# Three moves in the first part of a graph kernel: a check, a graph's split rows, and the turn of a state

## The chip, the core and the metric

The kernel runs on one core of one Trainium2 chip. The metric is the device time of one launch in microseconds (us). The engines are TensorE (PE in the profile; its weight loads are PEld), VectorE (DVE), ScalarE (ACT), GpSimd (POOL) and SyncE (SP), which here only issues DMAs. Each engine takes its own instructions in the order in which the program gives them, and waits on semaphores for the others.

## The reference

There are 16 graphs of 1024 nodes with 128 features. Two networks run one after the other; the change is in the part that computes the first network and, beside it, the adjacency of the second.

```python
# first network: four gated layers
h = x
for i in range(4):
    m = einsum('bjn,bjd->bnd', adj, h @ weight[i])
    gx, gh = m @ w_ih.T + b_ih, h @ w_hh.T + b_hh
    r = sigmoid(xr + hr); z = sigmoid(xz + hz); n = tanh(xn + r * hn)
    h = (1 - z) * n + z * h
x = layernorm(x + h * mask)

# second network: rows of adj are thinned one after the other
def step(carry, n):                  # for n = 0 .. 1023
    row = carry[n]
    num, rank = sum(row), cumsum(row)
    sf = where(num > 10, (num + 1) // 2, 1)
    rm = row & (rank % sf == 0)      # if num > 1
    carry[n] = row & ~rm
    carry[:, n] = carry[:, n] & ~rm  # later rows see it
# then three aggregations with adj * keep, batch norms, a head, layernorm
```

## The kernel before

The first part of the program (up to about 1470 us of 2624) holds two classes, whose instructions are woven into each other by hand: on PE, DVE, ACT, POOL and SP the order is that of the Python program.

`Gated` computes the first network. Two streams take turns, each with a graph of its own: stream 0 does a layer of its graph, then stream 1 a layer of its own, so that there are 64 layers in all. The state h lies turned, with features on partitions and the 1024 nodes along a row (`st.ht`, tile `h_h`), in two halves f = 0 and 1 of 512 nodes. A layer (`layer`, L1059) first aggregates: for each half 8 products with the high part of h by rows (`h_hi`) and 8 with the low part (`h_lo`), L1072, whose sum ScalarE copies to `h_ms` (L1075). Then come the gates of half 0 and half 1, all products at L1084. For each half: the reset gate's product, its sigmoid to `h_r` (L1093), the product ph, DVE's `(ph + b) * r` (L1099), the product px, DVE's sum (L1101), tanh (L1102), the update gate's product, its sigmoid to `h_z` (L1105), GpSimd's `z * h` (L1107), DVE's `(z - 1) * r` (L1108) and GpSimd's new half of h (L1109). The products rotate through five PSUM banks.

While one stream is in its layer, the other's new h is turned into rows for its next layer. `next_layer(f)` turns a half by four transposes into the tile `h_tr` (L1023), which has one PSUM buffer, and ScalarE copies that to `h_hi` (L1011); `rest(f)` subtracts on VectorE, from `h_tr` again, for `h_lo` (L1016). At a change of graph, `finish(f)` takes the place of this: it turns the half, ScalarE scales it (L1053), GpSimd adds it to x (L1055), and after the second half the sum is stored (L1057). `begin_rows` splits the next graph's x into `h_hi` on ScalarE (L1042) and `h_lo` on GpSimd (L1043, two of 512), and `begin` turns x (L1035).

`FixPoint` computes the thinning, in 32 blocks of 128 rows of four graphs. A block with index k cuts the columns that earlier blocks removed (`turn`, transposes at L722; `keep`, L727), ranks each row by a scan (`count`, L735), and takes the removals inside its diagonal by rounds. A round computes the row's parameters from the count (`params`, L694 to L701, six small DVE instructions into `f_q`), |scale * rank + bias| on ScalarE (`diag_u`, L886, four of 128) and the removals on VectorE (`removed`, L893, four, into `f_x`); `less` (L901 on PE, L903 on DVE) then gives the ranks without them, and the next round begins. After two such rounds `settle` computes ranks and parameters a third time, `wide_u` (ScalarE, L909 and L912) and `rows` (DVE, L863) write the four rows of 1024 and store them, and load the row of a later block. `last_u` and `check` do the diagonal a third time: `check` takes `removed` of it, four L893 from `f_u` in SBUF, and compares (L879) it with the round before. The result of the comparison goes into `bad`, which is looked at only at the end of the program.

`FixPoint.steps` is a generator of 20 places a block, and a layer takes ten of them: `aside(n)`, made by `beside` (L1141), runs the next place and then the jobs of the other stream that are listed under n. So a block lasts two layers. Places 0 to 3 stand in the aggregation and 4 behind it; 5 and 6 belong to half 0, 7, 8 and 9 to half 1. In the layers of stream 0 place 4 holds the fourth turn, keep and count, the first parameters and `diag_u`, and then `check` of the block before (L812); place 5 holds `removed`, 7 holds `less` with parameters and `diag_u`, 8 the second `removed`. In those of stream 1, places 1 to 4 hold `settle`, `wide_u` and `rows`, 5 the mask `f_both` (L775, four on VectorE and one on GpSimd) and the first turn, 6 the first count, 8 and 9 the second. `last_u` is handed back by place 4 and runs behind the first sigmoid.

The lines that say where the places stand in a half:

```python
nc.scalar.activation(r, pr, AF.Sigmoid, bias=bias(self.bs, 0))
if f == 1:
    aside(7)
elif later:
    later()
...
nc.scalar.activation(r, r, AF.Tanh, bias=bias(self.bi, 2))
aside(5 if f == 0 else 8)
```

Of the kernel before, what the change touches and what calls it, by code (L numbers as in the profile page):

```python
# [8 lines left out]
F32 = mybir.dt.float32  # L9
BF = mybir.dt.bfloat16  # L10
F16 = mybir.dt.float16
# [10 lines left out]
P = 128  # L22
# [604 lines left out]
class FixPoint:  # L627
# [17 lines left out]
    G = 4  # L645
# [40 lines left out]
    def params(self, num, r, rd=None):  # L686

        nc, G = self.nc, self.G
        q = self.small.tile([P, 4, G], F32, name="f_q")
        t = self.small.tile([P, 2, G], F32, name="f_t")  # L690
        h = self.sm[:, 2, r, :]
        ts, stt = nc.vector.tensor_scalar, nc.vector.scalar_tensor_tensor

        ts(h, num, 0.25 + 2.0 ** -14, HALVES, op0=ALU.mult, op1=ALU.add)  # L694
        ts(t[:, 1, :], num, 10.5, -3.0, op0=ALU.is_gt, op1=ALU.mult)
        ts(q[:, 0, :], num, 10.5, 1.0, op0=ALU.is_gt, op1=ALU.mult)
        stt(q[:, 1, :], h, HALVES, t[:, 1, :], op0=ALU.subtract, op1=ALU.mult)
        if rd:
            rd()
        stt(t[:, 0, :], h, HALVES, q[:, 0, :], op0=ALU.subtract, op1=ALU.mult)  # L700
        stt(q[:, 2, :], num, 1.5, t[:, 0, :], op0=ALU.is_le, op1=ALU.max)  # L701
        return q
# [34 lines left out]

    def steps(self):

        nc, G = self.nc, self.G
        for c in range(G):
            self.load(c)
        old = None
        for i, (k, b0) in enumerate(self.todo):
            diag = slice(k * P, k * P + P)

            yield  # L750
            if old:
                old.settle()
                old.wide_u(0)
            yield
            if old:
                old.wide_u(1)
                old.rows(0)
            yield
            if old:
                old.wide_u(2)  # L760
                old.rows(1)
            yield
            if old:
                old.rows(2)
                old.wide_u(3)
                old.rows(3)
            a = [self.loaded.pop((i, g)) for g in range(G)]
            pt = self.ps.tile([P, G, P], F32, name="f_pd")
            for g in range(G):
                nc.tensor.transpose(pt[:, g, :], a[g][:, diag], self.cst["ident"])  # L770
            yield old and old.last_u

            both = self.small.tile([P, G, P], BF, name="f_both")
            for g in range(G):
                nc.vector.tensor_mul(both[:, g, :], a[g][:, diag], pt[:, g, :])  # L775
            nc.gpsimd.affine_select(both, both, pattern=[[0, G], [1, P]], compare_op=ALU.is_gt, fill=0.0,
                                    base=0, channel_multiplier=-1)
            self.turn(i, 0)
            yield
            rank = self.two.tile([P, G, N], F16, name="f_rank")  # L780
            self.keep(i, a[0])
            self.count(i, 0, a[0], rank, pt)
            yield
            yield
            self.turn(i, 1)
            self.keep(i, a[1])
            yield
            self.count(i, 1, a[1], rank, pt)
            if i == 0:

                for c in range(G, self.LOTS):
                    self.load(c, nc.scalar)
            yield
            yield
            yield
            self.turn(i, 2)
            self.keep(i, a[2])
            self.count(i, 2, a[2], rank, pt)
            yield
            for g in range(G):  # L800
                self.read_back(i + 1, g)
            yield
            self.turn(i, 3)
            self.keep(i, a[3])
            self.count(i, 3, a[3], rank, pt)

            num = self.sm[:, 0, 0, :]
            nc.vector.tensor_scalar(num, rank[:, :, N - 1], 1.0, None, op0=ALU.mult)
            q = self.params(num, 0)
            u = self.diag_u(rank[:, :, diag], q)  # L810
            if old:
                old.check()  # L812
            yield
            x = self.removed(u, q, both)
            yield
            yield
            pd, num = self.less(x, rank, 1)
            rd = self.small.tile([P, G, P], F16, name="f_rd")
            q = self.params(num, 1, lambda: nc.vector.tensor_sub(rd, rank[:, :, diag], pd))
            u = self.diag_u(rd, q)  # L820
            yield
            x = self.removed(u, q, both)
            yield
            old = self.Block(self, i, a, rank, both, x)
            yield
        yield
        old.settle()
        for n in range(4):
            old.wide_u(n)
            if n < 3:  # L830
                yield
            old.rows(n)
        yield old.last_u
        yield
        old.check()

# [51 lines left out]
        return u  # L888

    def removed(self, u, q, both):  # L890
        x = self.small.tile([P, self.G, P], BF, name="f_x", bufs=3)
        for g in range(self.G):
            self.nc.vector.scalar_tensor_tensor(x[:, g, :], u[:, g, :], q[:, 2, g:g + 1], both[:, g, :],  # L893
                                                op0=ALU.is_equal, op1=ALU.mult)
        return x
# [21 lines left out]
class Gated:  # L917
# [141 lines left out]
    def layer(self, st, l, aside):  # L1059
# [6 lines left out]
        for f in range(2):  # L1066
# [7 lines left out]
            m = wk.tile([C, HF], F32, name="h_ms")  # L1074
            nc.scalar.copy(m, pm[f])  # L1075
            ms.append(m)
        later = aside(4)
        bias = lambda t, g: t[:, 3 * l + g:3 * l + g + 1]
        w = lambda t, g: t[:, l, g, :]

# [6 lines left out]
        for f in range(2):  # L1087
            h, m = st.ht[:, half[f]], ms[f]
            r = wk.tile([C, HF], F32, name="h_r")
            z = wk.tile([C, HF], F32, name="h_z")  # L1090
            zh = wk.tile([C, HF], F32, name="h_zh")
            pr = gate((w(self.wh, 0), h), (w(self.wi, 0), m))
            nc.scalar.activation(r, pr, AF.Sigmoid, bias=bias(self.bs, 0))  # L1093
            if f == 1:
                aside(7)
            elif later:
                later()
            ph = gate((w(self.wh, 2), h))
            nc.vector.scalar_tensor_tensor(r, ph, bias(self.bh, 2), r, op0=ALU.add, op1=ALU.mult)  # L1099
            px = gate((w(self.wi, 2), m))  # L1100
            nc.vector.tensor_add(r, px, r)  # L1101
            nc.scalar.activation(r, r, AF.Tanh, bias=bias(self.bi, 2))  # L1102
            aside(5 if f == 0 else 8)
            pz = gate((w(self.wh, 1), h), (w(self.wi, 1), m))
            nc.scalar.activation(z, pz, AF.Sigmoid, bias=bias(self.bs, 1))  # L1105

            nc.gpsimd.tensor_tensor(zh, z, h, ALU.mult)  # L1107
            nc.vector.scalar_tensor_tensor(r, z, 1.0, r, op0=ALU.subtract, op1=ALU.mult)  # L1108
            nc.gpsimd.tensor_tensor(h, zh, r, ALU.subtract)  # L1109
            aside(6 if f == 0 else 9)  # L1110
# [30 lines left out]
    def beside(self, st, ot, l, s, b0, steps):  # L1141


        before = l if s == 0 else l + 1
        if before in (0, L0):
            old = not (s == 0 and b0 == 0)
            new = not (s == 1 and b0 + 2 >= B)
            jobs = {5: [], 7: [], 9: []}
            nxt = ot.b + 2 if old else ot.b

            def begin():
                ot.b = nxt
                ot.begin(0)

            if old:
                jobs[5].append(lambda: ot.finish(0))
                jobs[7].append(lambda: ot.finish(1))
                jobs[0] = [lambda: ot.load_x(nxt)]
                for j in range(4, NB):
                    jobs.setdefault(j // 2 - 2, []).append(lambda j=j: ot.load_adj(nxt, j))  # L1160
            if new:
                jobs.setdefault(3 if old else 0, []).append(lambda: ot.begin_rows(nxt))
                jobs[9].append(begin)
        else:
            jobs = {5: [lambda: ot.next_layer(0), lambda: ot.rest(0)],
                    7: [lambda: ot.next_layer(1)], 8: [lambda: ot.rest(1)]}

        if l == L0 - 1:

            for j in range(4):  # L1170
                jobs.setdefault(4, []).append(lambda j=j: st.load_adj(st.b + 2, j))

        def aside(n):
            if n == 8:
                for job in jobs.get(n, ()):
                    job()
            later = next(steps, None)
            if n != 8:
                for job in jobs.get(n, ()):
                    job()  # L1180
            return later
        return aside


# [789 lines left out]
```

## Time and profile before

| | us |
|---|---|
| median of 3 runs | 2628.1 |
| lowest and highest | 2625.91, 2628.13 |
| profiled execution | 2626.24 |
| its span, from first to last instruction | 2624.5 |

Some rows of the page's table of groups, which the text below draws on:

| line, engine, tile | count | busy us | mean ns of one |
|---|---|---|---|
| L1084 PE h_g from h_h and h_wh | 768 | 418.4 | 628 |
| L1072 PE h_g from h_a and h_hi | 1024 | 280.0 | 415 |
| L735 DVE f_rank | 128 | 299.2 | 2343 |
| L863 DVE f_nr | 128 | 164.7 | 1289 |
| L1107 POOL h_zh | 128 | 219.1 | 1712 |
| L1109 POOL h_h | 128 | 164.3 | 1284 |
| L1102 ACT tanh to h_r | 128 | 92.5 | 723 |

How to read the lines that follow. A row of a timeline has the start and the length in us, engine, line, operation, output from input, the shape, a count, and in brackets the idle time of the engine before it and what ended it. Matmuls are pipelined, so that a row of several is a little longer than the time to the next row. A row of the view of waits has who waited for whom, the total in us, the number of waits and the longest. A row of the view of stretches has the stretch, its length, the busy time of PE, PEld, DVE, ACT and POOL, the clock that TensorE was granted (1.00 is full), the DMA engines' share and GB/s. Spans on POOL are rough.

### The profile page before, as it was taken

Reading aid. Unit: us, or ns where it says so; the run is one execution under the profiler, and the core shown is the slowest. Engines: PE = TensorE matmul, PEld = TensorE weight load, DVE = VectorE, ACT = ScalarE, POOL = GpSimd, SP = SyncE. Lnnn points to the kernel's source line nnn. Section 1 sums busy time; section 2 is a strip of 40 time slices with the busy share of each in tenths; the row PEclk is TensorE's granted clock in tenths of the full one; section 3 lists DMA queues with packets and bytes.
Section 4 is the critical chain, followed back from the end, with each engine's and each line's share of the span. In section 5 each row is a group of like instructions: output and inputs, shape, how many; then the busy total and the mean of one; then the engine's idle time right before and its main releaser. Section 6 shows DMA issues by size and latency. Waiting matters only on the chain.

```text
span 2624.5 us, 36126 instructions
## 1 busy us (share of the span) xinstructions
PE 2362.3 (90%) x12167; PEld 1590.7 (61%) x12167; DVE 1908.1 (73%) x4116; ACT 1404.2 (54%) x3228; POOL 1005.9 (38%) x938
## 2 busy tenths in 40 slices
PE   5998999989989999989899599999999989998875
PEld 4555555555555555555555367777777767777654
DVE  4887877888868888878788666666666566665667
ACT  3555455556455555555554455555555435545647
POOL 3335244353253442433532455544554434441000
PEclk9999999999999999999999899999999989999988
DMA  7236253363252352523630677667667366655304
GB/s 237 103 103 221 66 186 121 104 211 117 90 192 87 129 201 65 204 98 105 210 121 23 229 257 256 228 258 259 255 231 260 113 218 237 233 197 161 115 17 130
DMA packets 214391, 436.20 MB, mean 166 GB/s; under 512 B 59570, under 2 KB 80724, under 8 KB 214196
## 3 DMA queue, kind: packets, MB, share of 16 engines
q1 hardware_dynamic: 186756, 345.96, 37.9%
q0 software_dynamic: 23040, 83.90, 9.3%
q10 hardware_dynamic: 4400, 3.95, 0.5%
q8 instruction: 98, 1.61, 0.2%
q14 instruction: 97, 0.79, 0.1%
HBM read 324.49 MB, written 109.25 MB: 165 GB/s over the span
## 4 chain that ended last, share of the span: by engine, by line
PE 49%; DVE 22%; ACT 15%; DMA 6%; issue 6%; POOL 1%; ACTq 0%; DVEq 0%; SPq 0%; POOLq 0%
PE h_g L1084 12%; PE h_g L1072 12%; PE p_ag L1519 6%; DVE f_rank L735 3%; ACT s_junk L1359 3%; PE q_ag L1748 2%; ACT f_pd L886 2%; DMA h_x<-in_x_dram 2%; PE q_ob L1712 2%; DVE s_r L1370 2%; DMA p_a<-in_adj_dram 2%; DVE h_r L1099 1%; DVE h_r L1101 1%; PE p_u L1434 1%; PE h_tr L1023 1%
## 5 line engine op out<-in xcount | busy, mean ns | idle before, releaser
L1084 PE MATMUL h_g<-h_h,h_wh 128*128 128x512 f32 x768 | 418.4, 628 | 5.7 <-ACT h_ms L1075 5.5
L1084 PE MATMUL h_g<-h_ms,h_wi 128*128 128x512 f32 x768 | 405.0, 610 | 0.0
L1107 POOL TENSOR_TENSOR h_zh<-h_z,h_h 128x512 f32<-128x512 f32 x128 | 219.1, 1712 | 482.4 <-ACT h_z L1105 482.3
L735 DVE TENSOR_TENSOR_SCAN f_rank<-f_a,f_first,f_pd 128x1024 f16<-128x1024 f32 x128 | 299.2, 2343 | 3.0
L1449 POOL CAST p_b<-p_at 128x512 uint8<-128x512 f32 x256 | 213.1, 853 | 204.5 <-ACT p_at L1442 189.3
L1072 PE MATMUL h_g<-h_a,h_hi 128*128 128x512 f32 x1024 | 280.0, 415 | 0.0
L1084 PEld LDWEIGHTS h_g<-h_ms,h_wi 128*128 128x128 f32 x768 | 152.7, 199 | 197.3 <-issue 194.0
L1072 PE MATMUL h_g<-h_a,h_lo 128*128 128x512 f32 x1024 | 256.9, 393 | 0.0
L1442 ACT ACTIVATE p_at<-p_u,s_less 128x512 fp32r<-128x512 f32 x256 | 175.4, 686 | 146.3 <-PE p_u L1441 127.9
L863 DVE SCALAR_TENSOR_TENSOR f_nr<-f_u,f_q,f_a 128x1024 bf16<-128x1024 f16 x128 | 164.7, 1289 | 90.4 <-ACT f_u L912 73.6
L1072 PEld LDWEIGHTS h_g<-h_a,h_hi 128*128 128x128 f32 x1024 | 188.3, 188 | 57.5 <-issue 20.6
L1072 PEld LDWEIGHTS h_g<-h_a,h_lo 128*128 128x128 f32 x1024 | 189.9, 188 | 38.8
L1102 ACT ACTIVATE h_r<-h_r,h_bi 128x512 f32<-128x512 f32 x128 | 92.5, 723 | 193.3 <-DVE h_r L1101 192.7
L1084 PEld LDWEIGHTS h_g<-h_h,h_wh 128*128 128x128 f32 x768 | 135.7, 201 | 96.4 <-issue 79.6
L1455 DVE SCALAR_TENSOR_TENSOR p_junk<-p_a 128x1024 bf16<-128x1024 f32 x128 | 184.2, 1439 | 2.3
L1359 ACT ACTIVATE s_junk<-s_o 128x128 bf16<-128x128 f32 x384 | 113.6, 298 | 132.7 <-DVE s_o L1352 132.7
L1109 POOL TENSOR_TENSOR h_h<-h_zh,h_r 128x512 f32<-128x512 f32 x128 | 164.3, 1284 | 16.5 <-DVE f_tr L903 4.3
L909 ACT ACTIVATE f_u<-f_rank,f_q 128x128 f16<-128x128 f16 (+7 forms) x128 | 110.6, 867 | 90.1 <-DVE f_rank L849 90.1
L1075 ACT COPY h_ms<-h_g 128x512 f32<-128x512 f32 x128 | 73.9, 577 | 140.9 <-PE h_g L1072 98.5
L1440 PE MATMUL p_u<-ident_b,p_a 128*128 128x128 bf16 x1024 | 143.8, 221 | 4.4 <-DMA p_a<-in_adj_dram 4.4
L1441 PE MATMUL p_u<-ident_b,p_nr 128*128 128x128 bf16 x1024 | 143.8, 221 | 0.0
L1108 DVE SCALAR_TENSOR_TENSOR h_r<-h_z,h_r 128x512 f32<-128x512 f32 x128 | 105.6, 825 | 49.3 <-ACT h_z L1105 47.9
(241 smaller groups left out, 4988.2 us busy)
## 6 DMA issues: line engine op xcount, KB each, us to landing
h_a<-in_adj_dram POOLq DMA_DIRECT2D x128, 512.0 KB, 7.2
p_a<-in_adj_dram SPq DMA_DIRECT2D x128, 512.0 KB
f_a<-in_adj_dram SPq DMA_DIRECT2D x124, 512.0 KB
e_nr<-f_nr SPq DMA_DIRECT2D x128, 256.0 KB
p_nr<-e_nr SPq DMA_DIRECT2D x32, 1024.0 KB
s_at<-p_b SPq DMA_DIRECT2D x32, 512.0 KB
s_ag<-s_ag SPq DMA_DIRECT2D x64, 256.0 KB
q_agi<-s_ag SPq DMA_DIRECT2D x32, 512.0 KB
```

The costliest lines, as they stand in the source:

```text
L735: nc.vector.tensor_tensor_scan(out, a, other[:, 0, 0:1].to_broadcast([P, N]), start, op0=ALU.add, op1=ALU.bypass)
L863: nc.vector.scalar_tensor_tensor(nr, self.us[g], self.q[:, 2, g:g + 1], self.a[g], op0=ALU.not_equal, op1=ALU.is_ge)
L1072: nc.tensor.matmul(pm[f], part[:, j, :], st.adj[j][:, half[f]], start=(j == 0 and n == 0), stop=(j == NB - 1 and n == 1))
L1084: nc.tensor.matmul(pg, lhs, rhs, start=(i == 0), stop=(i == len(mm) - 1))
L1107: nc.gpsimd.tensor_tensor(zh, z, h, ALU.mult)
L1109: nc.gpsimd.tensor_tensor(h, zh, r, ALU.subtract)
L1359: self.nc.scalar.activation(junk, o[:, i, :], AF.Square, accum_out=ss[:, i:i + 1])
L1440: nc.tensor.matmul(pu[:, i * P:(i + 1) * P], a[:, blk, 1], ib, start=False, stop=False)
L1442: nc.scalar.activation(g["at"][:, j, cols], pu, AF.Relu, bias=self.less2)
L1449: self.nc.gpsimd.tensor_copy(g["b", f][:, j, :], g["at"][:, j, f * HF:(f + 1) * HF].bitcast(F32))
L1455: self.nc.vector.scalar_tensor_tensor(junk, a, 0.0, a, op0=ALU.is_gt, op1=ALU.not_equal, accum_out=self.bad[:, c:c + 1])
L1519: self.nc.tensor.matmul(pa, hi[:, j, :], at[:, j, f * HF:(f + 1) * HF], start=(start and n == 0), stop=(stop and n == len(js) - 1))
```

## The change

There are three edits and what they need of buffers.

- `check` of the block before goes from place 4 of stream 0's layer to its last place, 9, ahead of the making of the new `Block`. What it reads must live longer: `f_q` gets three buffers, `f_x` four; `f_rd` gets one.
- Places and jobs of half 0: `aside(5)` moves from behind the tanh to behind the reset gate's sigmoid, where `later` and `aside(7)` stood. With it move the first `removed` (stream 0's layers), `f_both` and the first turn (stream 1's), and the turn of the other stream's h with the copy to `h_hi`, or at a change of graph `finish(0)`. The subtraction for `h_lo` stays behind the tanh, under the name "rest". `last_u` is called in place 5 itself.
- `begin_rows` of the next graph goes from place 3 to place 7, behind `finish(1)`.

```diff
-        q = self.small.tile([P, 4, G], F32, name="f_q")
+        q = self.small.tile([P, 4, G], F32, name="f_q", bufs=3)
...
-            yield old and old.last_u
+            yield
+            if old:
+                old.last_u()
...
             u = self.diag_u(rank[:, :, diag], q)
-            if old:
-                old.check()
             yield
...
-            rd = self.small.tile([P, G, P], F16, name="f_rd")
+            rd = self.small.tile([P, G, P], F16, name="f_rd", bufs=1)
...
             x = self.removed(u, q, both)
             yield
+            if old:
+                old.check()
             old = self.Block(self, i, a, rank, both, x)
...
-        x = self.small.tile([P, self.G, P], BF, name="f_x", bufs=3)
+        x = self.small.tile([P, self.G, P], BF, name="f_x", bufs=4)
...
             nc.scalar.activation(r, pr, AF.Sigmoid, bias=bias(self.bs, 0))
-            if f == 1:
-                aside(7)
-            elif later:
-                later()
+            aside(5 + 2 * f)
...
             nc.scalar.activation(r, r, AF.Tanh, bias=bias(self.bi, 2))
-            aside(5 if f == 0 else 8)
+            aside("rest" if f == 0 else 8)
...
-                jobs.setdefault(3 if old else 0, []).append(lambda: ot.begin_rows(nxt))
+                jobs.setdefault(7 if old else 0, []).append(lambda: ot.begin_rows(nxt))
...
-            jobs = {5: [lambda: ot.next_layer(0), lambda: ot.rest(0)],
+            jobs = {5: [lambda: ot.next_layer(0)], "rest": [lambda: ot.rest(0)],
                     7: [lambda: ot.next_layer(1)], 8: [lambda: ot.rest(1)]}
...
         def aside(n):
-            if n == 8:
-                for job in jobs.get(n, ()):
-                    job()
-            later = next(steps, None)
-            if n != 8:
-                for job in jobs.get(n, ()):
-                    job()
-            return later
+            if n not in ("rest", 8):
+                next(steps, None)
+            for job in jobs.get(n, ()):
+                job()
+            if n == 8:
+                next(steps, None)
```

More of the change, by code (lines that the diff above doesn't have):

```diff
@@ L832, in steps @@
             old.rows(n)
-        yield old.last_u
+        yield
+        old.last_u()
         yield
@@ L1076, in layer @@
             ms.append(m)
-        later = aside(4)
+        aside(4)
         bias = lambda t, g: t[:, 3 * l + g:3 * l + g + 1]
```

## The prediction

> **What bounds the kernel now.** I read the page first, for the engines and TensorE's clock.
>
> ```profile
> span 2624.5 us, 36126 instructions
> PE 2362.3 (90%) x12167; PEld 1590.7 (61%) x12167; DVE 1908.1 (73%) x4116; ACT 1404.2 (54%) x3228; POOL 1005.9 (38%) x938
> ```
>
> TensorE looks like the bound, but in the first part (46 to 1446 us) it is busy for 1289 us of 1400. So I asked next what it waits for, in the view of waits for TensorE from 100 to 1400 us (total, times, longest).
>
> ```profile
> PE f_pd L901 <- DVE f_x L893: 64.8, 35, 3.1
> PE h_tr L1023 <- DVE h_lo L1016: 15.7, 28, 0.6
> PE h_tr L1023 <- ACT h_w L1053: 11.0, 14, 1.4
> ```
>
> It waits for VectorE. Third, TensorE's timeline at such a place, and the granted clock behind it (the number after the engines' busy times):
>
> ```profile
> 453.87 0.38 PE L901 MATMUL f_pd<-f_tri,f_x 128*128 128x128 bf16 x4 [1.39 <-DVE f_x L893]
> 454.88 0.63 PE L1023 MATMUL h_tr<-ident,h_h 128*128 128x128 f32 x4 [0.63 <-DVE h_lo L1016]
> ```
>
> ```profile
> 456.00:457.00 1.00, 1.00 (x3) 0.47 (x2) 0.86 (x5) 0.30 (x1) 0.92 (x2) 0.50 0.00 0
> ```
>
> Reading that view in steps of 0.25 us, I find 25 such stretches of half clock, each 3.41 or 3.42 us long, so each costs 1.71 us of work; each follows a stretch of the same length in which TensorE idled about 2 us or more.
>
> Last, VectorE's timeline over one block, which decides the forecast:
>
> ```profile
> 490.67 0.17 DVE L808 TENSOR_SCALAR f_tr<-f_rank 128x4 f32<-128x4 f16 x1
> ...
> 491.62 1.13 DVE L893 SCALAR_TENSOR_TENSOR f_x<-f_u,f_q,f_both 128x128 bf16<-128x128 f16 x4
> 492.78 0.69 DVE L879 SCALAR_TENSOR_TENSOR f_junk<-f_x 128x512 f16<-128x512 bf16 x1
> 493.40 0.08 DVE L879 DVE_READ_ACCUMULATOR f_junk<-f_x 128x1 f32 x1
> 494.06 0.75 DVE L1099 SCALAR_TENSOR_TENSOR h_r<-h_g,h_bh,h_r 128x512 f32<-128x512 f32 x1 [0.57 <-ACT h_r L1093]
> 494.91 0.69 DVE L1101 TENSOR_TENSOR h_r<-h_g,h_r 128x512 f32<-128x512 f32 x1
> 495.52 1.11 DVE L893 SCALAR_TENSOR_TENSOR f_x<-f_pd,f_q,f_both 128x128 bf16<-128x128 f32 x4
> ...
> 503.65 1.42 DVE L1108 SCALAR_TENSOR_TENSOR h_r<-h_z,h_r 128x512 f32<-128x512 f32 x1
> 505.00 0.15 DVE L903 TENSOR_TENSOR f_tr<-f_rank,f_pd 128x4 f32<-128x4 f16 x1
> ```
>
> L808 follows the fourth rank scan (call its start E); the second L903 after it opens the settling of the block. The next L808 stands at 533.06. So the round is E to L903, 14.33 us, and L903 to the next E, 28.06. Over 30 rounds the first leg is 14.3 to 14.9 us in the 23 without a change of graph (14.3 without half clock) and 17.3 to 20.3 in the other seven; the second is 27.9 to 31.3. In the second leg VectorE waits only for ScalarE, whose work hangs on the same L903, except 0.47 us for h_hi and 0.17 for TensorE's f_tr. The check (L893 on f_u, and L879, 1.86 us) is free where it stands: after it VectorE still waits 0.57 us for the sigmoid. So VectorE with ScalarE is as tight a ring as TensorE.
>
> **The Trainium skill.** "TensorE: Matmul & The Clock Gate", Part 1, says that TensorE's clock halves after an idle window of about 3.4 us; the trace agrees on the length (3.41), but about 2 us idle of it suffices, and I use that. "SBUF — State Buffer", Who interferes with whom, says that a VectorE instruction with two SBUF inputs and a GpSimd instruction that reads SBUF exclude each other, whoever comes first. The trace agrees. Above, L1108 took 1.42 instead of 0.69 us because GpSimd's L1107 had begun at 503.25. And at the end of the first part the check happens to stand beside GpSimd's work:
>
> ```profile
> 1460.25 1.71 POOL L1107 TENSOR_TENSOR h_zh<-h_z,h_h 128x512 f32<-128x512 f32 x1
> ...
> 1460.76 4.23 DVE L893 SCALAR_TENSOR_TENSOR f_x<-f_u,f_q,f_both 128x128 bf16<-128x128 f16 x4
> 1462.04 1.27 POOL L1109 TENSOR_TENSOR h_h<-h_zh,h_r 128x512 f32<-128x512 f32 x1
> 1463.26 1.31 POOL L1055 TENSOR_TENSOR h_x<-h_x,h_w 128x512 f32<-128x512 f32 x1
> ...
> 1465.02 0.69 DVE L879 SCALAR_TENSOR_TENSOR f_junk<-f_x 128x512 f16<-128x512 bf16 x1
> ```
>
> Four products of 1.13 us took 4.23: one passes between two of GpSimd's instructions.
>
> **The change part by part**, in the block above, times from E.
>
> *f_x ahead of the gate.* diag_u runs from +0.80 to +2.74 (491.47, 1.94 us). f_x now follows at once: +2.77 to +3.89. L1099 and L1101, behind it, take 0.85 and 0.69: to +5.35. L1016 follows, to +5.96. In before it ended at +6.88 (496.86 and 0.69). TensorE comes to L901 at +4.49 (496.69 less 1.53 idle). It no longer waits for f_x there, but the turn of h behind it has one PSUM buffer and waits for L1016: after L901's 0.22 us it idles from +4.71 to about +6.1, 1.4 us in place of 2.3. A gain for TensorE of 0.9 us, and half of the slow stretches may go.
>
> *h turned earlier.* Four transposes (0.44 us from start to start) go ahead of the L1084 of f = 0; TensorE's sum is unchanged. L1099 has them hidden: it waits for f_x, not for that product. On ScalarE h_hi (0.57) goes ahead of tanh, into time in which it waited 1.61 us for L1101. Tanh comes at +5.4, z at +6.0 (before: +6.06), L1108 and the first L903 at +7.4, as before (498.07). From there VectorE's order is unchanged up to L1108 of f = 1, which ends at about +14.4. So VectorE's ring gains nothing here.
> In the other layer f_both (0.87 us) goes ahead of L1099 and delays it by 0.82; the 0.47 wait for h_hi goes, as does a little of others: the first scan comes 0.3 later, of which the 0.17 wait for f_tr takes half. I take +0.15.
>
> *The check in the last place.* It now stands between L1108 (f = 1) and L903 on VectorE, and L1107 and L1109 (1.28 us each alone) run on GpSimd just then: in this block L1109 began at 505.25, behind L1108. From +14.33 one product passes (+14.6), L1109 takes 1.29 (+15.9), three more products 0.8 (+16.7), L879 with its read 0.74 (+17.4). Where L1108 comes first, L1107 waits for it and both of GpSimd's stand ahead; the sum is within 0.3 of this. So L903 comes at +17.4 in place of +14.33: 3.1 us later. Everything of the second leg is queued behind it (wide_u, four rows with their stores, counts); the f_a loads behind those stores are for the block after next. Nothing takes the delay up: 3.1 + 0.15 = 3.2 a round, 23 x 3.2 = 74 us. Where slow stretches go, 0.6 each comes back (14.9 to 14.3): for half of the blocks, 7 us. Left: 67.
>
> *Rows split four places on.* Two copies on ScalarE (1.14 us) leave the place where they waited for x's load (61.5 us in all, 14 times) ahead of h_ms and wide_u; I take 2.2 us off the second leg of seven rounds (30.8 to 31.3, where 28.6 would fit its neighbours). On GpSimd L1043 (two of 1.25) now stands behind L1055 and the store's issue, ahead of L1107. The check of that layer then has up to three more instructions to pass, and TensorE's second pass waits for h_lo. I put its L903 at E + 20.8 against 18.6 on the mean of the seven: plus 2.2. Seven times minus 2.2 and plus 2.2: nothing. The x load is in by then; the loads issued on GpSimd behind L1043 come earlier, and nobody waited for them.
>
> *Buffers.* One more f_q and f_x, one less f_rd, whose last reader is a block back: no wait. SyncE's order in this part is the same.
>
> The sum: 2626.2 (the profiled execution, 1.9 below the median of 2628.1) plus 67 is 2693, against the median 2695. If the slow stretches stay, as TensorE now idles longer in all, it is 74 and 2702. I take the middle, **2698**.
>
> **The rivals.**
> 1. The check costs only its 1.86 us, because it gets the port first: L903 at +16.2, plus 2.0 a round, 46 us: 2672, and down to 2645 if it hides partly in the 0.67 us for which L903 waits for TensorE in some blocks. Against it: the 4.23 us. Chance 0.17.
> 2. It costs as at the end of the part, one GpSimd instruction for each product: 5.0 us, +19.3, 5.2 a round, 120 us, with 14 more at changes of graph: 2762. Against it: an ordinary block has only two such instructions there. Chance 0.09.
> 3. Faster: the second leg has slack of 3 us that I read as work, so the check is free and TensorE alone counts. Then 30 x 0.9 = 27, 25 x 1.71 = 43 for the slow stretches, and 7 x 2.2 = 15 for the rows go: 2541, or 2562 where half of the stretches stay, which I take. It decides if the fourth scan doesn't come later against TensorE. For it: TensorE is busy for 92% of this part; against it: the scan waits for TensorE for 0.17 us only. Chance 0.09.
> 4. Gain and loss cancel: 2628. Chance 0.05.
> The forecast has 0.60, with a range of its own of 2675 to 2730.
>
> **How the numbers follow.** A change of 0.2% (5 us) is what a measurement of this kernel tells from none. Slower: 0.60 + 0.17 + 0.09 = 0.86; same 0.05; faster 0.09. From 2645 to 2745 lie the forecast, the first rival and the nearer half of the second: 0.81.
>
> **What would show it.** Right: L903 of the settling comes 17 us or more after E; the products on f_u take 2.5 us or more for four; TensorE waits at L901 less, and at the second turn of h for h_lo more; the round is 45 to 46 us where it was 42.4. Wrong: L893 on f_u at 1.1 us for four, or a round that stays at 42 while L903 is late. If h_hi still waits for x's load, the rows step is wrong.

## The result, and the profile after

| | before | after |
|---|---|---|
| median of 4 runs, us | 2628.11 | 2708.12 |
| lowest to highest | 2625.91 to 2631.12 | 2705.03 to 2709.78 |
| profiled execution | 2626.24 | 2705.03 |

The changed kernel takes 1.0302 times as long (95% interval 1.0284 to 1.032). 2698 was forecast. From here the line numbers of the changed kernel count. Those of the gates stand three lower than before: DVE's L1108 is L1105, GpSimd's L1107 and L1109 are L1104 and L1106, and the sigmoid for `h_z`, which was L1105, is L1102. L808 is L807; L893, L903, L901, L1016, L1023, L1042 and L1043 keep their numbers. The texts on check_only and rows_only, which are edits of the kernel before, and on check_psum have the numbers L1107, L1108 and L1109 again.

The page of the changed kernel, its busy times and the chain that ended last:

```profile
span 2703.3 us, 36186 instructions
PE 2384.5 (88%) x12150; PEld 1589.7 (59%) x12167; DVE 1980.8 (73%) x4116; ACT 1396.2 (52%) x3228; POOL 993.7 (37%) x938
...
DVE 38%; PE 27%; ACT 22%; issue 8%; DMA 3%; POOL 0%; DVEq 0%; SPq 0%; ACTq 0%; POOLq 0%
```

TensorE has 22 us more of busy time, the span 79 us more. The chain ran for 49% over TensorE before and for 22% over VectorE; now it is 27% and 38%. Of before:

```profile
PE 49%; DVE 22%; ACT 15%; DMA 6%; issue 6%; POOL 1%; ACTq 0%; DVEq 0%; SPq 0%; POOLq 0%
```

These shares alone do not tell the loss: check_back, below, has 33% and 39% and is faster than before, and check_only, the slowest version, has 42% and 27%. TensorE's waits from 100 to 1500 us (total, times, longest):

```profile
PE h_tr L1023 <- DVE h_lo L1016: 82.6, 45, 2.1
PE f_pd L901 <- DVE f_x L893: 22.3, 30, 1.8
...
PE h_g L1072 <- POOL h_lo L1043: 9.6, 7, 2.0
```

Over the same 100 to 1500 us the kernel before has 67.9 us at L901 and 16.2 at the turn of h, so the first wait fell and the second rose. The third is new. VectorE's timeline in the block that the prediction took:

```profile
513.41 0.17 DVE L807 TENSOR_SCALAR f_tr<-f_rank 128x4 f32<-128x4 f16 x1
...
516.25 1.13 DVE L893 SCALAR_TENSOR_TENSOR f_x<-f_pd,f_q,f_both 128x128 bf16<-128x128 f32 x4 [1.81 <-ACT f_pd L886]
517.29 0.74 DVE L1096 SCALAR_TENSOR_TENSOR h_r<-h_g,h_bh,h_r 128x512 f32<-128x512 f32 x1
...
526.39 1.42 DVE L1105 SCALAR_TENSOR_TENSOR h_r<-h_z,h_r 128x512 f32<-128x512 f32 x1
527.73 2.20 DVE L893 SCALAR_TENSOR_TENSOR f_x<-f_u,f_q,f_both 128x128 bf16<-128x128 f16 x4
529.96 0.69 DVE L879 SCALAR_TENSOR_TENSOR f_junk<-f_x 128x512 f16<-128x512 bf16 x1
530.58 0.08 DVE L879 DVE_READ_ACCUMULATOR f_junk<-f_x 128x1 f32 x1
530.58 0.16 DVE L903 TENSOR_TENSOR f_tr<-f_rank,f_pd 128x4 f32<-128x4 f16 x1
```

and GpSimd's at the end of it:

```profile
525.98 1.27 POOL L1104 TENSOR_TENSOR h_zh<-h_z,h_h 128x512 f32<-128x512 f32 x1 [2.62 <-ACT h_z L1102]
527.97 1.28 POOL L1106 TENSOR_TENSOR h_h<-h_zh,h_r 128x512 f32<-128x512 f32 x1 [0.72 <-DVE h_r L1105]
```

The check stands between L1105 and L903, and its four products took 2.20 us where 1.13 sufficed before. One passed as L1106 began at 527.97; three came after its end at 529.25. L903 stands at E + 17.17, where it stood at E + 14.33.

The first leg is the time from E to the second L903, the second leg the time from there to the next E. A half-clock stretch is a stretch in which TensorE's granted clock is 0.50. The 30 rounds are counted from 0, which is the second block. Means over the 23 ordinary rounds and the 7 with a change of graph, read from VectorE's timelines, all versions of this study together (the last column is explained in the last section; each ratio is to runs of before on the same chip):

| version | median us | ratio to before, 95% interval | first leg | second leg | first, change of graph | second, change of graph | half-clock stretches in 30 rounds |
|---|---|---|---|---|---|---|---|
| before | 2628.1 | | 14.68 | 29.26 | 18.59 | 28.91 | 23 |
| after | 2708.1 | 1.0302 [1.0284, 1.032] | 17.29 | 29.36 | 21.23 | 28.72 | 24 |
| check_only | 2743.8 | 1.0433 [1.0416, 1.0451] | 18.12 | 30.30 | 19.85 | 29.56 | 55 |
| split_only | 2620.0 | 0.9961 [0.995, 0.9973] | 14.42 | 29.01 | 19.40 | 28.99 | 21 |
| rows_only | 2637.6 | 1.0039 [1.0025, 1.0053] | 14.53 | 29.48 | 19.51 | 29.42 | 21 |
| check_back | 2614.4 | 0.9946 [0.9929, 0.9962] | 14.41 | 29.25 | 18.42 | 28.72 | 19 |
| rows_back | 2688.0 | 1.0223 [1.0206, 1.024] | 17.34 | 29.09 | 18.95 | 28.72 | 24 |
| no_check | 2613.3 | 0.9946 [0.9929, 0.9962] | 14.42 | 29.23 | 18.36 | 28.71 | 17 |
| check_psum | 2675.6 | 1.0181 [1.0164, 1.0198] | 16.37 | 29.29 | 20.39 | 28.72 | 22 |
| check_behind | 2614.1 | 0.9944 [0.9928, 0.9961] | 14.35 | 29.24 | 18.36 | 28.72 | 12 |
| rows_5 | 2680.7 | 1.02 [1.0183, 1.0217] | 17.27 | 28.90 | 18.85 | 28.72 | 18 |
| back_rows_5 | 2601.6 | 0.9899 [0.9882, 0.9915] | 14.42 | 28.90 | 17.51 | 29.00 | 17 |

After against before: 23 x (2.61 + 0.10) + 7 x (2.64 - 0.19) = 79.5 us, and the profiled executions differ by 78.8. The legs hold the whole loss, and nearly all of it lies in the first leg.

### The profile page after: what moved, and what is told of

Same layout as the page of the kernel before. It is cut to its first block, busy times and chain, and to the rows that moved or that the text cites. A ratio compares the mean times of both kernels' runs of the same rounds, so it can differ in the third digit from the quotient of the medians.

```text
span 2703.3 us, 36186 instructions
## 1 busy us (share of the span) xinstructions
PE 2384.5 (88%) x12150; PEld 1589.7 (59%) x12167; DVE 1980.8 (73%) x4116; ACT 1396.2 (52%) x3228; POOL 993.7 (37%) x938
## 4 chain that ended last, share of the span: by engine, by line
DVE 38%; PE 27%; ACT 22%; issue 8%; DMA 3%; POOL 0%; DVEq 0%; SPq 0%; ACTq 0%; POOLq 0%
DVE f_rank L735 7%; PE p_ag L1514 6%; DVE h_r L1105 5%; DVE f_x L893 4%; ACT f_pd L886 4%; ACT f_u L909 3%; PE h_g L1084 3%; ACT s_junk L1354 3%; PE h_g L1072 3%; ACT f_u L912 3%; PE q_ag L1743 2%; DVE h_r L1098 2%; DVE h_r L1096 2%; ACT h_z L1102 2%; DVE f_a L727 2%
## 5 line engine op out<-in xcount | busy, mean ns | idle before, releaser
L1084 PE MATMUL h_g<-h_h,h_wh 128*128 128x512 f32 x768 | 408.3, 614 | 0.0
L1104 POOL TENSOR_TENSOR h_zh<-h_z,h_h 128x512 f32<-128x512 f32 x128 | 207.1, 1618 | 517.3 <-ACT h_z L1102 517.3
L1072 PE MATMUL h_g<-h_a,h_hi 128*128 128x512 f32 x1024 | 293.9, 428 | 2.6 <-ACT h_hi L1011 2.6
L1072 PE MATMUL h_g<-h_a,h_lo 128*128 128x512 f32 x1024 | 263.6, 399 | 9.9 <-POOL h_lo L1043 9.6
L1072 PEld LDWEIGHTS h_g<-h_a,h_hi 128*128 128x128 f32 x1024 | 194.3, 195 | 67.0 <-issue 20.6
L1105 DVE SCALAR_TENSOR_TENSOR h_r<-h_z,h_r 128x512 f32<-128x512 f32 x128 | 156.2, 1220 | 88.6 <-ACT h_z L1102 88.4
L863 DVE SCALAR_TENSOR_TENSOR f_nr<-f_u,f_q,f_a 128x1024 bf16<-128x1024 f16 x128 | 164.1, 1284 | 76.0 <-ACT f_u L912 67.2
L1106 POOL TENSOR_TENSOR h_h<-h_zh,h_r 128x512 f32<-128x512 f32 x128 | 164.4, 1284 | 36.4 <-DVE h_r L1105 25.2
L1023 PE MATMUL h_tr<-ident,h_h 128*128 128x128 f32 x512 | 81.3, 282 | 104.2 <-DVE h_lo L1016 85.7
L1023 PEld LDWEIGHTS h_tr<-ident,h_h 128*128 128x128 f32 x512 | 57.9, 143 | 154.9 <-issue 129.3
```

Source lines behind the costliest of these rows:

```text
L863: nc.vector.scalar_tensor_tensor(nr, self.us[g], self.q[:, 2, g:g + 1], self.a[g], op0=ALU.not_equal, op1=ALU.is_ge)
L1072: nc.tensor.matmul(pm[f], part[:, j, :], st.adj[j][:, half[f]], start=(j == 0 and n == 0), stop=(j == NB - 1 and n == 1))
L1084: nc.tensor.matmul(pg, lhs, rhs, start=(i == 0), stop=(i == len(mm) - 1))
```

## The experiments

### One edit at a time

In the texts from here, "the port" is short for what the prediction cited: a VectorE instruction with two SBUF inputs and a GpSimd instruction that reads SBUF exclude each other.

check_back and no_check take the check out of the last place: the first puts it back behind `diag_u` (place 4), the second leaves it out but for the last block's.

```diff
             u = self.diag_u(rank[:, :, diag], q)
+            if old:
+                old.check()          # check_back only
...
             x = self.removed(u, q, both)
             yield
-            if old:
-                old.check()
             old = self.Block(self, i, a, rank, both, x)
```

> The changed kernel with its check of the block before put back behind diag_u, the other two edits kept. Theory (the check's place costs 2.6 us a round on the VectorE and ScalarE ring, and the whole loss of 79 us is this): the check is free there, so the first leg of ordinary rounds falls from 17.3 back to 14.3 to 14.7 us, that of graph-change rounds from 21.2 to about 18.6, and the time is 2615 to 2628 us. Rival (the earlier turn of h and f_both, or the split of rows, have a part of the loss): legs stay longer than before's, time 2640 to 2690 us.

> The changed kernel without the check of the block before in the blocks' loop (only the last block's check stays; the flags are set to zero once). Theory (the check is free at place 4, all of its price in the last place is place and port): within 4 us of the version with the check put back, 2610 to 2617 us, first leg 14.3 to 14.5. Rival (the check at place 4 costs some of its 1.86 us still): 2570 to 2605 us.

2614.4 and 2613.3 us: with the check at place 4 the changed kernel is faster than the one before, and the check costs nothing there that can be measured. (2614.4 is just under the range expected.) Its move costs 2708.1 - 2614.4 = 93.7 us with the other two edits in place. Without any check the time is the same as with it at place 4, so all of these 94 us come from where it stands. Both versions keep the change's buffer counts, so these are no part of the loss.

check_only is the kernel before with the check alone moved (the lines of `check` and the three buffer counts of the change's diff).

> The kernel before with the check alone moved to the last place (and its buffers). Theory: it has the whole loss by itself, first leg 17.0 to 17.5 us, four products on f_u about 2.2 us, time 2690 to 2710 us. Rival (place without the port): products 1.13 us, first leg 16.5 us, time about 2670 us. Rival (the loss comes from the edits together): under 2660 us.

2743.8 us: more than the whole change, and more than any theory gave. The first leg was put at 17.0 to 17.5 and is 18.12, the products at 2.2 and they take 3.28 in the same block of this version: L1108 waited for `h_z`, it began just ahead of GpSimd's L1107, and so both of GpSimd's instructions meet the products. VectorE and GpSimd there:

```profile
540.46 0.69 DVE L1108 SCALAR_TENSOR_TENSOR h_r<-h_z,h_r 128x512 f32<-128x512 f32 x1 [0.17 <-ACT h_z L1105]
541.07 3.28 DVE L893 SCALAR_TENSOR_TENSOR f_x<-f_u,f_q,f_both 128x128 bf16<-128x128 f16 x4
```

```profile
540.50 1.80 POOL L1107 TENSOR_TENSOR h_zh<-h_z,h_h 128x512 f32<-128x512 f32 x1 [3.64 <-ACT h_z L1105]
542.38 1.29 POOL L1109 TENSOR_TENSOR h_h<-h_zh,h_r 128x512 f32<-128x512 f32 x1
```

That `h_z` is late goes with TensorE's half clock. In before, six of the 23 ordinary rounds have no half-clock stretch in the first leg, and there L1107 begins 12.6 us after E; in the other 17 it begins at 13.1 to 13.6. In check_only each of the 23 has one or two, L1107 begins at 13.1 to 14.7, and the products take 3.3 us. In after, whose L1104 is the same instruction, nine have one stretch and it still begins at 12.7, and in the six of split_only (below) with one at 12.6 to 12.7; only round 6 of after, with two, is late (13.8), and there the products take 3.27 us and the first leg 18.29. So with the earlier turn a single stretch in the first leg costs little, and check_only is without it.

The second leg of check_only grew too, by 1.04 us, and 55 half-clock stretches stand where 23 stood. Its four ordinary rounds without a stretch in the second leg (30.5 us) are as long there as in before. Against rows_back (below), which differs from it by the earlier turn alone, check_only has 31 stretches more; at 1.71 us of work each that is 53 us, and the two times differ by 55.8. The sizes agree and the rounds sort by the stretches, but the clock was not changed by itself, so it is not shown to be the cause of the whole difference.

split_only has the earlier turn alone; rows_only has `begin_rows` at place 7 alone; rows_back is the changed kernel with `begin_rows` at place 3.

```diff
-                jobs.setdefault(7 if old else 0, []).append(lambda: ot.begin_rows(nxt))
+                jobs.setdefault(3 if old else 0, []).append(lambda: ot.begin_rows(nxt))
```

> The kernel before with the earlier turn alone (places and jobs of half 0, and the buffers); check at place 4 and begin_rows at place 3 as before. Theory (rows at place 7 cost about 9 us in whichever order, by L1108 on the shared port): 2614 less 9, about 2605 us; first leg of ordinary rounds 14.3 to 14.5, of graph-change rounds 18.0 or less. Rival (the rows' place costs only in the order of before): 2612 to 2617 us. Rival (the turn gains nothing of itself, it only pairs with the rows): 2622 us or more.

> The kernel before with begin_rows alone moved to place 7. Theory (the wait for x's load goes, 2 us, but the two L1043 on GpSimd now hold L1108 of the second half by 2.5 us through the shared port): the fourth row L863 comes about 2 us earlier after L903, L1108 takes about 3.2 instead of 0.7 us, the second leg of rounds 2, 10, 18 and 26 stays at 30.8 to 31.3 us, time 2622 to 2632 us. Rival (in the changed kernel it was the check or the earlier turn that took the gain): second legs fall to 28.8 us, time 2610 to 2618 us.

> The changed kernel with begin_rows back at place 3. Theory (with the earlier turn the rows' place moves time between the legs, second leg of rounds 2, 10, 18 and 26 about 30.0 in place of 30.9, first leg at a change of graph about 1 us more): 2700 to 2716 us, within 0.3 per cent of the changed kernel. Rival (the rows' place has a large part of the loss, or of the gain that the changed kernel has over the check alone at 2744): below 2695 or above 2725 us.

rows_only has this edit the other way round, on the kernel before; split_only has it on check_back.

The turn gains 8 us (its runs lie between 2610.8 and 2626.0). The 2605 that split_only was expected at missed, and 2620.0 lies between its two rivals; its first legs at a change of graph stayed at 19.40, where 18.0 or less was expected. rows_only missed its range as well, at 2637.6, with second legs of 31.7 us in rounds 2, 10, 18 and 26: the rows' place costs 9 us alone (2628.8 for the runs of before beside it). With the turn and the check at place 4, no loss from it can be told (2620.0 and 2614.4, intervals that overlap). rows_back missed its range too: at 2688.0 its rival came true. So the rows' place, which the forecast put at nothing, costs 20.1 us in the changed kernel. The steps add up in this order: turn -8.1, check +68.0, rows +20.1, together +80.0.

### Place or port

check_psum keeps every instruction of the check in its place, but the four products read PSUM for their second operand.

```diff
-            again = fix.removed(self.u, self.q, self.both)
+            again = fix.small.tile([P, fix.G, P], BF, name="f_x", bufs=4)
+            for g in range(fix.G):
+                fix.nc.vector.scalar_tensor_tensor(again[:, g, :], self.u[:, g, :], self.q[:, 2, g:g + 1],
+                                                   fix.tr[:, 0, :], op0=ALU.is_equal, op1=ALU.mult)
...
-            fix.nc.vector.scalar_tensor_tensor(junk, again, 1.0, self.x, op0=ALU.mult, op1=ALU.not_equal,
+            fix.nc.vector.scalar_tensor_tensor(junk, again, 1.0, again, op0=ALU.mult, op1=ALU.not_equal,
```

> The changed kernel; the four products of the check read f_tr in PSUM in place of f_both in SBUF as second operand, and L879 compares the result with itself, so that the check no longer tests anything; instructions and places are the same. Theory (shared port): the four products take 1.13 us in place of 2.2, the first leg falls by 0.8 to 1.1 us to 16.2 to 16.5, the time by 18 to 33 us to 2675 to 2690 us. Rival (place alone; GpSimd's part is incidental): the products go to 1.13 us but L903 stays where it is, 2700 to 2710 us.

VectorE's timeline in the same block (lines behind the diff stand three higher, the products are L879), and GpSimd's:

```profile
516.82 1.42 DVE L1108 SCALAR_TENSOR_TENSOR h_r<-h_z,h_r 128x512 f32<-128x512 f32 x1
518.16 1.11 DVE L879 SCALAR_TENSOR_TENSOR f_x<-f_u,f_q,f_tr 128x128 bf16<-128x128 f16 x4
519.30 0.93 DVE L882 SCALAR_TENSOR_TENSOR f_junk<-f_x 128x512 f16<-128x512 bf16 x1
```

```profile
518.40 1.28 POOL L1109 TENSOR_TENSOR h_h<-h_zh,h_r 128x512 f32<-128x512 f32 x1 [0.72 <-DVE h_r L1108]
```

The products run at 1.11 us across L1109; L882, which still has two inputs in SBUF, waits for its end (519.68) and takes 0.93 instead of 0.69. The first leg is 16.37: of the check's 2.88 us on it (17.29 less check_back's 14.41), 0.92 is the port at the products, and 1.96 is the place, with the 0.24 us that L882 still waits. The time falls by 32.5 us, at the upper edge of what was expected. "SBUF — State Buffer", Who interferes with whom, says that a VectorE instruction with at most one SBUF input does not contend with GpSimd, outside the modes in which it uses two ports; these products agree (1.11 against 2.20 us in the same place).

check_behind moves the check past `settle` and the first `wide_u`: a few small instructions later in VectorE's order.

```diff
             if old:
                 old.settle()
                 old.wide_u(0)
+                if prev:
+                    prev.check()
...
-            if old:
-                old.check()
-            old = self.Block(self, i, a, rank, both, x)
+            prev, old = old, self.Block(self, i, a, rank, both, x)
```

> The changed kernel with the check moved on once more, from just ahead of settle to just behind it and the first wide_u (L879 writes over its first input, which saves a buffer; f_q has four and f_x five buffers). Theory (the price is what stands behind the check on the ring, not its lateness): behind settle VectorE waits 0.92 us for f_u and 0.6 us more before the third row, and GpSimd only issues DMAs, so the four products take 1.13 us, the first leg goes back to 14.3 to 14.5 (18.4 at a change of graph), and of 1.86 us at most 0.9 stays on the second leg: 2614 to 2641 us. Rival (a late check costs its 1.86 us on the ring wherever it stands): 2665 us or more.

```profile
500.03 0.16 DVE L903 TENSOR_TENSOR f_tr<-f_rank,f_pd 128x4 f32<-128x4 f16 x1
...
501.96 1.13 DVE L893 SCALAR_TENSOR_TENSOR f_x<-f_u,f_q,f_both 128x128 bf16<-128x128 f16 x4
503.13 0.69 DVE L879 SCALAR_TENSOR_TENSOR f_x<-f_x 128x512 bf16<-128x512 bf16 x1
503.75 0.08 DVE L879 DVE_READ_ACCUMULATOR f_x<-f_x 128x1 f32 x1
503.75 3.88 DVE L864 SCALAR_TENSOR_TENSOR f_nr<-f_u,f_q,f_a 128x1024 bf16<-128x1024 f16 x3
508.23 1.28 DVE L864 SCALAR_TENSOR_TENSOR f_nr<-f_u,f_q,f_a 128x1024 bf16<-128x1024 f16 x1 [0.61 <-ACT f_u L912]
```

This is VectorE in the same block. 2614.1 us: the price is gone, all of it. In the changed kernel VectorE waits after `settle` for ScalarE's `f_u` (0.9 to 1.0 us for the first row, 0.6 before the second and before the fourth); here three rows run without a gap and the fourth waits 0.61 as ever, so the second leg stays at 29.24. The check is no earlier than in the changed kernel. Two things differ: the instructions behind it on VectorE wait for ScalarE in any case, and GpSimd computes nothing then, so that the products take 1.13 us.

### Where the gain of the rows went

The wait for x's load (61.5 us before) no longer shows in the changed kernel. In the layer of stream 1 at a change of graph, the fourth row (L863) in before:

```profile
189.61 0.17 DVE L903 TENSOR_TENSOR f_tr<-f_rank,f_pd 128x4 f32<-128x4 f16 x1 [0.67 <-PE f_pd L901]
...
199.77 1.28 DVE L863 SCALAR_TENSOR_TENSOR f_nr<-f_u,f_q,f_a 128x1024 bf16<-128x1024 f16 x1 [2.63 <-ACT f_u L912]
```

and in after, with what followed:

```profile
196.62 0.16 DVE L903 TENSOR_TENSOR f_tr<-f_rank,f_pd 128x4 f32<-128x4 f16 x1
...
204.75 1.28 DVE L863 SCALAR_TENSOR_TENSOR f_nr<-f_u,f_q,f_a 128x1024 bf16<-128x1024 f16 x1 [0.60 <-ACT f_u L912]
...
216.12 3.20 DVE L1105 SCALAR_TENSOR_TENSOR h_r<-h_z,h_r 128x512 f32<-128x512 f32 x1 [0.77 <-ACT h_z L1102]
```

```profile
214.99 2.53 POOL L1043 TENSOR_TENSOR h_lo<-h_x,h_hi 128x512 fp32r<-128x512 f32 x2
217.48 1.28 POOL L1104 TENSOR_TENSOR h_zh<-h_z,h_h 128x512 f32<-128x512 f32 x1
```

The row came at L903 + 8.13 instead of + 10.16: the 2 us were there. Eleven us later L1105, 0.69 us of work, waited for L1043 and then for L1104, and gave 2.5 back. rows_only showed the same on the kernel before (L1108 took 3.18 us), and its fourth row came at L903 + 8.13 too. In the layer of stream 0, 25 us on, it is worse. VectorE and GpSimd of after:

```profile
241.64 4.35 DVE L1105 SCALAR_TENSOR_TENSOR h_r<-h_z,h_r 128x512 f32<-128x512 f32 x1 [2.16 <-ACT h_z L1102]
245.91 2.21 DVE L893 SCALAR_TENSOR_TENSOR f_x<-f_u,f_q,f_both 128x128 bf16<-128x128 f16 x4
```

```profile
241.66 2.52 POOL L1043 TENSOR_TENSOR h_lo<-h_x,h_hi 128x512 fp32r<-128x512 f32 x2
244.13 1.30 POOL L1104 TENSOR_TENSOR h_zh<-h_z,h_h 128x512 f32<-128x512 f32 x1
```

In rows_back L1105 takes 0.69 here and the check 3.79; the first leg of these rounds is 18.95 against 21.23. rows_5 puts `begin_rows` at place 5 of the changed kernel, ahead of `finish(0)`; back_rows_5 does so with the check at place 4.

```diff
-                jobs.setdefault(7 if old else 0, []).append(lambda: ot.begin_rows(nxt))
+                jobs.setdefault(5 if old else 0, []).insert(0, lambda: ot.begin_rows(nxt))
```

> The changed kernel with begin_rows at place 5 ahead of finish(0), so that the two L1043 fall where GpSimd is idle. Theory (the gain of the rows' step was eaten by L1105, held by L1043): L1105 of the second half of the layers at a graph change takes 0.7 us in place of 3.2, second leg of rounds 2, 10, 18 and 26 goes from 30.9 to about 29, first leg of graph-change rounds from 21.2 to about 20; time 2680 to 2697 us. Rival (ScalarE's two copies in place 5 hold tanh and z back by as much): 2703 us or more.

> The changed kernel with the check back behind diag_u and begin_rows at place 5. Theory: the gains add, 2590 to 2606 us. Rival (ScalarE's copies in place 5 cost as much as L1105's wait): 2612 us or more.

VectorE and GpSimd of rows_5 in the layer of stream 1:

```profile
210.69 1.68 DVE L1105 SCALAR_TENSOR_TENSOR h_r<-h_z,h_r 128x512 f32<-128x512 f32 x1 [1.82 <-ACT h_z L1102]
218.15 0.69 DVE L1105 SCALAR_TENSOR_TENSOR h_r<-h_z,h_r 128x512 f32<-128x512 f32 x1 [0.77 <-ACT h_z L1102]
```

```profile
208.09 2.50 POOL L1043 TENSOR_TENSOR h_lo<-h_x,h_hi 128x512 fp32r<-128x512 f32 x2
```

L1043 is done at 210.59, and L1105 of the second half takes 0.69 us. Rounds 2, 10, 18 and 26 have second legs of 29.85 in place of 30.9, the first leg at a change of graph is 18.85 in place of 21.23, and the time falls by 27.4 us. ScalarE no longer waits for x there, so x is loaded by then, and place 7 was the wrong end of the free time. TensorE's wait for L1043's `h_lo` (9.6 us in after) is gone with it; what part of the gain is that was not separated. back_rows_5, at 2601.6 us, is 1.0% under the kernel before and the fastest version run.

## Why the prediction was right, and where not

The main step held. The check was put at +3.1 us on the first leg of ordinary rounds and 71 us in all; between split_only and rows_back it is 17.34 less 14.42, 2.92 us, and 68.0 us of time. L903 was forecast at E + 17.4 in the block shown; it stands at + 17.17. The mechanism was right in its parts: one product, L1106, three products, then L879; nothing of the second leg takes the delay up. Only the bound given for the products was off: 2.5 us or more, and they take 2.2. The prediction's own working, from +14.33 to +16.7, has 2.4; 2.5 is passed only where L1105 comes ahead of L1104, as in round 6 (3.27). The round in the block shown is 45.25 us, inside the 45 to 46 forecast.

The first rival put the check at its bare duration and the time at 2672. check_psum is nearly that world: 2675.6. The second, one GpSimd instruction for each product, is seen nowhere in the rounds; the nearest is 3.8 us for four at a change of graph, in check_only, rows_back and rows_5. The third, that the second leg had slack, falls: the legs carry the whole loss.

f_x ahead of the gate: L901's wait fell and the turn's rose as forecast, with 1.76 us in the block where 1.4 was forecast. The gain was taken as 7 us for the stretches less 0.15 x 23 for the other layer, about 3.5; split_only gains 8.1. But half of the stretches did not go (21 stand in split_only and 24 in after, where 23 stood). What went is their effect on the first leg: over 14.7 in 14 of the 23 ordinary rounds before, 14.3 to 14.5 in all but one of check_back. So the turn, of which the prediction said that VectorE's ring gains nothing, brought the gain there.

The step that failed is "Rows split four places on": "Seven times minus 2.2 and plus 2.2: nothing." The size of the plus was right: 21.23 less 18.95 is 2.28. The minus was not: second legs of the seven rounds rose, from a mean of 30.16 to 30.90 (rounds 2, 10, 18, 26) and from 27.02 to 28.35 (rounds 6, 14, 22), rows_back to after. With 7 x 2.28 = 16.0, 4 x 0.74 = 3.0 and 3 x 1.33 = 4.0 that is 23 us; 20.1 was measured. The gain was also read from too many rounds: the prediction has 30.8 to 31.3 us for the second legs of all seven, but only rounds 2, 10, 18 and 26 have that before; 6, 14 and 22 have 28.75. The prediction had seen that L1043 would share the port at its new place, and charged it to the check in one of the two layers. It also meets L1105, in both layers, fourteen times and not seven; in the layer without a check it ate the gain, and in the other it is L1105 and not the check that pays (4.35 us for 0.69; the check stays at 2.21). The saved 2 us were real in the trace, and the turn alone had already taken part of them: second legs of 30.8 to 31.3 before are 29.95 to 30.2 in split_only.

The sum came near in part by luck. The rows' 20 us were missing; on the other side the check was put 3 us too dear, and the turn's gain 5 us too small. The sum was 67 and the forecast, which went halfway to 74, was 70; 80 was measured.

## What to carry to other kernels

Book-keeping that nobody waits for should stand behind the instruction that opens the next chain, in a gap that another engine makes, and not ahead of it: a few instructions in the order were worth 94 us here. When a GpSimd instruction with SBUF inputs is moved, list every VectorE instruction with two SBUF inputs that can meet it at the new place, in each kind of layer, and not only the one the change is about. An edit measured alone says little where edits share a gap: the check cost 115, 68, 79 or 94 us and the rows' place 9, about nothing or 20, by what stood around them.

## What the hardware showed beside

Whether VectorE gets a turn between GpSimd instructions that follow each other without a gap is not one rule here. L1105, begun with the first L1043 at 241.64, took 4.35 us and ended after two L1043 and L1104; at all 14 such places of after it ended behind L1104. But in before, in the first half of the same layer, L1108 ended 0.55 us after L1055 and 1.1 us ahead of the end of L1107, which followed L1055 without a gap:

```profile
230.89 1.28 DVE L1108 SCALAR_TENSOR_TENSOR h_r<-h_z,h_r 128x512 f32<-128x512 f32 x1 [1.36 <-ACT h_z L1105]
```

```profile
230.35 1.27 POOL L1055 TENSOR_TENSOR h_x<-h_x,h_w 128x512 f32<-128x512 f32 x1 [4.30 <-ACT h_w L1053]
231.58 1.71 POOL L1107 TENSOR_TENSOR h_zh<-h_z,h_h 128x512 f32<-128x512 f32 x1
```

The prediction's "one passes between two of GpSimd's instructions" came from lines of the same kind, and it held for the check's products. It failed for L1105 at L1043; what makes the difference is not shown.

TensorE's half-clock stretches, summed over the 30 rounds from steps of 0.25 us, come to a whole number of 3.41 us in all twelve traces: 12 to 55 of them. Their number alone does not give the time. check_behind has 12 and check_back 19 at the same time (2614.1 and 2614.4): with the earlier turn a single stretch in an ordinary round's first leg lengthens it by about 0.2 us (17.36 for 17.17 in after), and without it by up to 0.6 (14.9 for 14.33 in before). In check_only, with 55, they go with a loss of about their size.
